# First layer of a graph network: its own-row term and offsets move into the matmul groups

## The chip, the core and the metric

The kernel runs on one core of one Trainium2 chip. The metric is device time in microseconds (us) of one launch. TensorE is written PE, VectorE DVE, ScalarE ACT, GpSimd POOL and SyncE SP. PE, DVE and ACT compute, POOL issues the gathers, SP issues most of the other transfers. Each engine works through its own instructions in the order of the program and stops at the first one whose inputs are not there.

## The reference, cut to what matters

A table of 12500 nodes with 256 features goes through a normalization, then through a graph network of three layers over 200000 edges, an attention and a mixture of experts. The change lies in the first layer of the graph network, and in how it hands its result to the second:

```python
def _sage_conv(x, src, dst, Wl, bl, Wr, num_nodes):
    msg = x[src]
    s = segment_sum(msg, dst, num_nodes)
    cnt = segment_sum(ones, dst, num_nodes)
    agg = s / maximum(cnt, 1.0)[:, None]
    return agg @ Wl.T + bl + x @ Wr.T

h = _sage_conv(xn, src, dst, Wl0, bl0, Wr0, n)
h = leaky_relu(h, 0.01)
h = _sage_conv(h, src, dst, Wl1, bl1, Wr1, n)
...
```

The **mean** term is `agg @ Wl.T`, the **own row** is `x @ Wr.T`, the **offset** is `bl`.

## The kernel before, in words

**Data.** The nodes form 98 blocks of 128 rows (`NB`), taken in 27 groups of four blocks, at the end of the order of two. The edges are sorted by target into slots of 128. In layers 1 and 2 the sums are taken after the linear product, so each layer stores two tables for the next: `y` (the product with `Wl`, which is gathered) and `z` (the product with `Wr` plus the offset, the own row). `y_tab[0]` is the normalized table itself.

**A layer** is `on_the_way_of` (L1672). Its loop (L1891) takes four slots in each step: POOL gathers four slots of messages (L1709) into a ring of 32 tiles, ACT makes the matrices `hots` that sort 128 messages into 128 targets (L1698, L1700), and PE multiplies them into the running sums `acc` (L1729). A gather into a slot waits until the product 32 slots earlier has read it. When all slots of a block have been added, `take_up` (L1742) divides the sums by the counts on DVE (L1755 to L1759) and clears them (L1767).

**Work put between the slots.** `stage(0)` takes the queue `soon`, which holds the finished groups (`products`, L697); `stage(1)` takes the queue `later`, in layer 0 the generator `first_products` (L731). Each is a generator: a step of the loop runs it to its next `yield 0.0`, one call of each per step, and a credit of `SHARE` paces the second by the costs that are yielded. So the order of instructions on every engine is written out when the program is built. Six blocks with most edges are summed differently: POOL, DVE and PE count edges per pair of nodes (`counted`, L1527) and PE multiplies the counts with the whole table (`sums`, L1651). They come in the middle and in the last third of the layer.

**`first_products`** loads a group of normalized rows, transposes it on PE (`turned`, L682, copied by ACT at L691), stores the transposed rows in `xT_tab` (L737), multiplies them with `Wr` (L744, PSUM tile `p_z`), adds the first offset on DVE (L746) and stores `z_tab[0]` (L749). `load_z` (L1788) reads that back as `h` before the group's last block is taken up.

**`products`** transposes the mean, multiplies it with `Wl` (L707, tile `p_l`), adds `h` on DVE (L710), applies the leaky ReLU on DVE (L711: the larger of `h` and 0.01 `h`), transposes the result and calls `linear`. **`linear`** (L252) multiplies with both matrices of the next layer at once into one PSUM tile `p_mm` of 512 columns (L259); ACT copies the left half (L268), DVE adds the offset to the right half (L269), and both halves are stored (L280, L281). In layer 1 the same function is called with `parts` and splits the left half in three; that branch keeps its work.

In layer 0 all PSUM tiles but `acc` and `whole` share three banks (`OneTag`, L1663). The SBUF tag `t_b` (two buffers) holds the transposed mean, the transposed `h` and the two tiles `yz` in turn; `t_a` (two buffers) holds `z0`; `h` has three buffers.

The attention already adds an offset by a product: `ones3` (3 x 128 ones, bf16) times `bo3` (three bf16 rows whose sum is the f32 offset), L845, in front of two f32 products at L847. The three rows are made at the start (L337 to L345).

Of the kernel before, what the change touches and what calls it, by code (L numbers as in the profile page):

```python
# [56 lines left out]
P = 128  # L57
D = 256
# [30 lines left out]
def gps_kernel(ctx: ExitStack, tc: tile.TileContext, x, src, dst, wlr, bl, wq, wk, wv,  # L89
# [75 lines left out]
    bo_tab = dram.tile([3, D], BF, name="bo_tab")  # L165
    xa_tab = dram.tile([NB * P, D], F32, name="xa_tab")


# [6 lines left out]
    def rows(t, b, n):  # L175

        return t[b * P:(b + n) * P, :].rearrange("(j p) d -> p j d", p=P)
# [9 lines left out]

    def spread(t):

        return bass.AP(tensor=t.tensor, offset=t.offset,  # L190
                       ap=[[0, P], [D, t.shape[0]], [1, D]])


    ident = consts.tile([P, P], F32, name="ident")
# [9 lines left out]
    nc.vector.memset(eps, EPS)  # L204


    bl_sb = consts.tile([P, 3, D], F32, name="bl_sb")
    bo3 = consts.tile([3, D], BF, name="bo3")
# [43 lines left out]
    def linear(psum, bufs, pool, layer, w, hT, b, n, parts=None):  # L252

        for j0 in range(0, n, 2):
            ps = []
            for j in range(j0, min(j0 + 2, n)):
                p = psum.tile([P, 2 * D], F32, name="p_mm", tag="p_mm", bufs=bufs)
                for k in range(2):
                    nc.tensor.matmul(p, hT[:, k, j * P:(j + 1) * P], w[:, k, :],  # L259
                                     start=(k == 0), stop=(k == 1))  # L260
# [24 lines left out]

    with ExitStack() as first:
# [47 lines left out]
        nc.scalar.dma_start(edges[E:E + P, :], fill)  # L334

        nc.sync.dma_start(bl_sb, spread(bl))
        bo = sort.tile([1, D], F32, name="bo")  # L337
        nc.sync.dma_start(bo, b_out)
        bo_parts = sort.tile([1, 3, D], BF, name="bo_parts")
        for i in range(3):  # L340
            nc.vector.tensor_copy(bo_parts[:, i, :], bo)
            if i < 2:
                nc.vector.tensor_sub(bo, bo, bo_parts[:, i, :])
        nc.sync.dma_start(bo_tab.rearrange("(o t) d -> o t d", o=1), bo_parts)
        nc.sync.dma_start(bo3, bo_tab)  # L345


        nxt_i = sort.tile([EP, 1], I32, name="nxt_i")
# [295 lines left out]
    def addresses(table, s, n, held, engine, pitch):  # L644
# [2 lines left out]
            max_val=(held - 1) * pitch, skip_runtime_bounds_check_because="clamped above")  # L647
        return at

    def finish(layer, b, n, sums, inv, work, h):  # L650


        r0 = NB - b - n
        if layer == 0:
            nc.vector.tensor_scalar(inv[:, r0:r0 + n], sums[:, :n, D], 1.0, None, op0=OP.max)
            nc.vector.reciprocal(inv[:, r0:r0 + n], inv[:, r0:r0 + n])
            m = work.tile([P, G, D], F32, name="mean", tag="t_a")
        for j in range(n):
            i = n - 1 - j
            if layer == 0:  # L660
                nc.vector.tensor_scalar(m[:, j, :], sums[:, i, :D], inv[:, r0 + i:r0 + i + 1], None,
                                        op0=OP.mult)
            else:
                nc.vector.scalar_tensor_tensor(h[:, j, :], sums[:, i, :D],
                                               inv[:, r0 + i:r0 + i + 1], h[:, j, :],
                                               op0=OP.mult, op1=OP.add)
        nc.vector.memset(sums if layer == 0 else sums[:, :n, :D], 0.0)
        if layer == 0:
            return m
        if layer == 2:  # L670
            nc.sync.dma_start(rows(z_tab[2], b, n), h[:, :n, :])
        return h
# [24 lines left out]
    def products(layer, b, n, m, h, work, psum, parts=None):  # L697


        if layer == 0:  # L700
            mT = yield from turned(m, n, work, psum, "t_b")
            for j0 in range(0, n, 2):
                nj = min(2, n - j0)
                p = psum.tile([P, 2, D], F32, name="p_l", tag="p_mm", bufs=2)
                for j in range(j0, j0 + nj):
                    for k in range(2):
                        nc.tensor.matmul(p[:, j - j0, :], mT[:, k, j * P:(j + 1) * P],  # L707
                                         wlr_sb[:, 0, k, :D], start=(k == 0), stop=(k == 1))
# [22 lines left out]
    def first_products(b, n, work, psum):  # L731

        xn = work.tile([P, G, D], F32, name="xn", tag="t_d")
        nc.sync.dma_start(xn[:, :n, :], rows(y_tab[0], b, n))
        yield 0.0
        xT = yield from turned(xn, n, work, psum, "t_c")
        nc.sync.dma_start(xT_tab[:, :, b * P:(b + n) * P], xT[:, :, :n * P])  # L737
        z = work.tile([P, G, D], F32, name="z0", tag="t_a")
        for j0 in range(0, n, 2):
            nj = min(2, n - j0)  # L740
            p = psum.tile([P, 2, D], F32, name="p_z", tag="p_mm", bufs=2)
            for j in range(j0, j0 + nj):
                for k in range(2):
                    nc.tensor.matmul(p[:, j - j0, :], xT[:, k, j * P:(j + 1) * P],  # L744
                                     wlr_sb[:, 0, k, D:], start=(k == 0), stop=(k == 1))
            nc.vector.tensor_add(z[:, j0:j0 + nj, :], p[:, :nj, :],  # L746
                                 bl_sb[:, 0:1, :].to_broadcast([P, nj, D]))
# [86 lines left out]
    def attended(b, n, work, psum):  # L834
# [6 lines left out]
        for j0 in range(0, n, 2):  # L841
            nj = min(2, n - j0)
            p = psum.tile([P, 2, D], F32, name="p_a", tag="p_mm", bufs=2)
            for j in range(j0, j0 + nj):
                nc.tensor.matmul(p[:, j - j0, :], ones3, bo3, start=True, stop=False)  # L845
                for k in range(2):
                    nc.tensor.matmul(p[:, j - j0, :], xT[:, k, j * P:(j + 1) * P], m2_sb[:, k, :],  # L847
                                     start=False, stop=(k == 1))
            nc.vector.tensor_add(xa[:, j0:j0 + nj, :], xa[:, j0:j0 + nj, :], p[:, :nj, :])
            yield 0.9 * nj  # L850
# [473 lines left out]
    def one_by_one():  # L1324

        with ExitStack() as stack:
# [6 lines left out]
            with ExitStack() as inner:  # L1333
# [5 lines left out]
                for layer in range(3):  # L1339
# [8 lines left out]
                    for b, n in falling:  # L1348
# [5 lines left out]
                        h = work.tile([P, G, D], F32, name="h")  # L1354
                        nc.sync.dma_start(h[:, :n, :], rows(z_tab[layer], b, n))
# [316 lines left out]
    def on_the_way_of(layer, table, last, work, psum, inv, msgs, a, c, e):  # L1672
# [109 lines left out]
        def load_z(g):  # L1782
            b, n = falling[g]
            if g >= group_of[FEWER] and not e:
                zs[g] = c.work.tile([P, 2, D], F32, name="h_c", bufs=PAIRS)
            else:
                zs[g] = work.tile([P, G, D], F32, name="h", bufs=3)
            nc.sync.dma_start(zs[g][:, :n, :], rows(z_tab[layer], b, n))  # L1788

        def ask(g):  # L1790

# [197 lines left out]
```

## Time and profile before

| what | value |
| --- | --- |
| five runs | 6685.4 to 6712.27 us, median 6687.13 us |
| profiled execution, its own time | 6699.41 us |
| its span in the profile | 6697.6 us |
| mean clock that PE was granted | 0.883 |
| layer 0 | about 190 us to 2345 us of the span |
| `first_products` in it | 192 us to 640 us |
| `products` of layer 0 | 302 us to 2336 us |

A row of the group view names line, engine and operation, the tile written, the tiles read, the shape (partitions x elements), the count, the busy time in us, the mean ns of one, and the idle time ahead of it with what ended that idle time. An f32 product of the program is two MATMULs in the trace (392 for 196 at L744), a bf16 product is one. "The chain" is the chain of work that ended last, followed back from the end; its shares are shares of the time in the window asked for. PEclk is the share of the full clock that PE was granted.

### The profile page before, as it was taken

What the parts mean: (1) busy time and instruction counts of PE and PEld (TensorE: products, weight loads), DVE (VectorE), ACT (ScalarE), POOL (GpSimd) and SP (SyncE); (2) the same over time, 40 slices, a digit from 0 to 9 for tenths busy, and PEclk for the clock granted to TensorE, in tenths of its full rate; (3) what the DMA queues carried; (4) which work ended last, traced back from release to release, by engine and by line L of the source; (5) the groups of instructions that cost most, each with busy time, mean ns of one, the idle gap of its engine ahead of it and who ended that gap; (6) DMA issues with size and microseconds to landing.
All of it is one profiled execution on the core that took longest, in us unless ns stands there. A gap on an engine that the chain in (4) does not pass through costs nothing.

```text
span 6697.6 us, 77095 instructions
## 1 busy us (share of the span) xinstructions
PE 5107.5 (76%) x23443; PEld 3722.4 (56%) x23443; DVE 2179.4 (33%) x6539; ACT 2252.7 (34%) x5187; POOL 4077.1 (61%) x4243
## 2 busy tenths in 40 slices
PE   1567677678888867877878776588889877888878
PEld 0446455455776645655555554356666545666556
DVE  6426647464000112222111100134444423333333
ACT  3324333344333334444333333122232222322223
POOL 1566667676666565665655666566666655666563
PEclk9879889889999979888888887689999888999889
DMA  6546334445777555555666654555666645666442
GB/s 200 159 136 201 109 111 128 123 151 177 228 225 226 178 163 185 182 175 178 208 219 207 213 165 138 169 178 178 196 183 201 181 131 159 187 184 182 148 148 81
DMA packets 752785, 1154.11 MB, mean 172 GB/s; under 512 B 109813, under 2 KB 582800, under 8 KB 752134
## 3 DMA queue, kind: packets, MB, share of 16 engines
q0 software_dynamic: 218320, 616.79, 31.3%
q1 hardware_dynamic: 516489, 512.20, 23.6%
q10 hardware_dynamic: 17578, 20.04, 0.9%
q8 instruction: 221, 3.62, 0.2%
q14 instruction: 177, 1.45, 0.1%
HBM read 940.73 MB, written 207.91 MB: 171 GB/s over the span
## 4 chain that ended last, share of the span: by engine, by line
PE 59%; issue 12%; another core or an unknown queue 11%; DVE 7%; ACT 6%; DMA 3%; POOL 2%; SPq 0%; ACTq 0%; DVEq 0%; POOLq 0%
PE acc L1729 19%; PE whole L1651 8%; PE p_h L1246 7%; PE p_y L1214 7%; PE p_mm L259 4%; ACT hots L1698 2%; PE p_n L1561 2%; PE p_tr L682 2%; PE p_a L847 1%; POOL msg L1709 1%; PE p_l L707 1%; ACT hots L1700 1%; PE p_z L744 1%; PE p_b L946 1%
## 5 line engine op out<-in xcount | busy, mean ns | idle before, releaser
L1709 POOL DMA_INDIRECT msg<-y,src_of x2480 | 2427.9, 979 | 1472.2 <-issue 653.8
L1709 POOL DMA_INDIRECT msg_parts<-y_parts,src_of x1404 | 1400.0, 997 | 726.0 <-issue 362.1
L1729 PE MATMUL acc<-msg,hots 128*128 128x257 f32 (+1 forms) x4960 | 1428.4, 410 | 501.2 <-issue 290.8
L1729 PEld LDWEIGHTS acc<-msg,hots 128*128 128x128 f32 x4960 | 975.8, 205 | 747.4 <-issue 421.4
L1698 ACT ACTIVATE hots<-cols,dst_of 128x128 f32<-128x128 f32 x2480 | 789.3, 391 | 740.2 <-remote 319.9
L1651 PE MATMUL whole<-y_c,count 128*128 128x256 f32 x2744 | 754.7, 396 | 60.9 <-issue 43.9
L1729 PE MATMUL acc<-msg_parts,hots 128*128 128x256 bf16 x4212 | 655.0, 284 | 126.7 <-issue 77.7
L1214 PE MATMUL p_y<-w_sb,hT 128*128 128x256 f32 x2368 | 599.1, 396 | 83.6 <-DVE x L1201 31.5
L1729 PEld LDWEIGHTS <-hots 128*128 128x128 bf16 x4212 | 424.3, 102 | 423.3 <-issue 296.4
L1246 PE MATMUL p_h<-turned,w_sb 128*128 128x512 f32 (+1 forms) x1344 | 620.9, 588 | 28.5 <-issue 17.1
L1651 PEld LDWEIGHTS whole<-y_c,count 128*128 128x128 f32 x2744 | 539.3, 200 | 160.4 <-issue 82.8
L1248 ACT ACTIVATE hT<-p_h,b_sb 128x512 f32<-128x512 f32 (+1 forms) x336 | 211.5, 636 | 1007.5 <-PE p_h L1246 434.5
L1214 PEld LDWEIGHTS p_y<-w_sb,hT 128*128 128x128 f32 x2368 | 448.6, 199 | 162.0 <-issue 37.5
L1700 ACT ACTIVATE hots<-hots,ones 128x512 f32<-128x512 f32 x620 | 447.4, 722 | 20.2
L1703 DVE TENSOR_TENSOR hots<-cols,dst_of 128x512 bf16<-128x512 f32 x351 | 240.7, 687 | 638.4 <-PE acc L1729 351.5
L1201 DVE SCALAR_TENSOR_TENSOR x<-p_y,comb,x 128x256 f32<-128x256 f32 x592 | 257.0, 476 | 515.4 <-PE p_y L1214 176.4
L259 PE MATMUL p_mm<-wlr_sb,turned 128*128 128x512 f32 x784 | 383.1, 632 | 52.6 <-issue 19.4
L1561 PE MATMUL p_n<-dst_hot,src_hot 128*128 128x256 bf16 x2058 | 299.3, 290 | 112.5 <-issue 75.1
L1246 PEld LDWEIGHTS p_h<-turned,w_sb 128*128 128x128 f32 x1344 | 255.2, 208 | 190.1 <-issue 165.0
L1561 PEld LDWEIGHTS <-src_hot 128*128 128x128 bf16 x2058 | 212.0, 104 | 200.1 <-issue 133.3
L691 ACT COPY turned<-p_tr 128x512 f32<-128x512 f32 (+1 forms) x204 | 105.5, 546 | 535.6 <-PE p_tr L682 255.2
L1541 DVE TENSOR_SCALAR src_hot<-nums,source_of 128x384 bf16<-128x384 uint16 x693 | 226.7, 327 | 177.5 <-remote 122.3
(386 smaller groups left out, 4633.9 us busy)
## 6 DMA issues: line engine op xcount, KB each, us to landing
count<-counts SPq DMA_DIRECT2D x294, 256.0 KB
y_c<-y SPq DMA_DIRECT2D x294, 256.0 KB
msg<-y,src_of POOLq DMA_INDIRECT x2480
counts<-counts_sb SPq DMA_DIRECT2D x96, 384.0 KB
h<-z SPq DMA_DIRECT2D x66, 512.0 KB
z<-yz SPq DMA_DIRECT2D x98, 256.0 KB
xT<-xT_tab SPq DMA_DIRECT2D x44, 512.0 KB
msg_parts<-y_parts,src_of POOLq DMA_INDIRECT x1404
```

What stands on the lines that cost most here:

```text
L259: nc.tensor.matmul(p, hT[:, k, j * P:(j + 1) * P], w[:, k, :], start=(k == 0), stop=(k == 1))
L1201: nc.vector.scalar_tensor_tensor(xt[:, j, :], p[:, j - j0, :], comb[:, j, i:i + 1], xt[:, j, :], op0=OP.mult, op1=OP.add)
L1214: nc.tensor.matmul(p[:, j - j0, :], hT[:, k, j * P:(j + 1) * P], e.w2[:, i, k, :], start=(k == 0), stop=(k == 1))
L1246: nc.tensor.matmul(p_h[:, :n * P], e.w1[:, i, k, m * P:(m + 1) * P], tT[:, k, :n * P], start=(k == 0), stop=(k == 1))
L1541: nc.vector.tensor_scalar(src_hot[:, i, :], self.nums, source[:, c:c + 1], None, op0=OP.is_equal)
L1561: nc.tensor.matmul(p[:, t, :], s_hot[:, (t0 + t) * P:(t0 + t + 1) * P], d_hot, start=(i == 0), stop=(i == len(mine) - 1))
L1651: nc.tensor.matmul(acc[:, h * D:(h + 1) * D], c[:, j, h * P:(h + 1) * P], y[:, j, :], start=False, stop=True, skip_group_check=True)
L1698: nc.scalar.activation(hot[:, i, :], cols, AF.Abs, bias=dst_of[:, s + i:s + i + 1], scale=-1.0)
L1700: nc.scalar.activation(hot[:, :n, :], hot[:, :n, :], AF.Relu, bias=ones[:, 0:1], scale=-1.0)
L1703: nc.vector.tensor_tensor(hot[:, :n, :], cols.rearrange("p (o c) -> p o c", o=1).to_broadcast([P, n, P]), dst_of[:, s:s + n].rearrange("p ...
L1709: got = nc.gpsimd.indirect_dma_start(out=msgs[s % held] if e else msgs[s % held][:, :D], out_offset=None, in_=y_parts if e else y_tab[laye ...
L1729: got = nc.tensor.matmul(sums, hot, msgs[s % held][:, k * D:k * D + w], start=False, stop=True, skip_group_check=True)
```

## The change

- `first_products` ends with the store of `xT_tab`. Its product with `Wr`, the addition and the store of `z_tab[0]` go.
- `load_h` reads, in layer 0, the group's transposed rows from `xT_tab` in place of `z_tab[0]`, into the same three buffers.
- `products` of layer 0 builds one PSUM group for each block: the offset as `ones3` x `rows3`, two products of the own row, two of the mean. ACT writes 0.01 times the PSUM tile to a new tile `h0` (tag `t_a`), DVE takes the larger of PSUM and `h0`. The pair of blocks now ends with `yield 0.0`, so a group of four takes one more call of `stage(0)`.
- `linear`, called without `parts`, adds the offset as `ones3` x `rows3` between its two products of a block, and ACT copies all 512 columns. The addition on DVE goes there.
- At the start, the two offsets and the attention's offset are split together as one row of 768 in place of 256, with one more load; `bl_sb` keeps the third offset alone.

```diff
@@ linear
                 for k in range(2):
                     nc.tensor.matmul(p, hT[:, k, j * P:(j + 1) * P], w[:, k, :],
                                      start=(k == 0), stop=(k == 1))
+                    if k == 0 and not parts:
+                        nc.tensor.matmul(p[:, D:], ones3, rows3[:, layer, :], start=False,
+                                         stop=False, skip_group_check=True)
...
-                nc.scalar.copy(y3[:, j, 0, :] if parts else yz[:, j, :D], p[:, :D])
-                nc.vector.tensor_add(yz[:, j, D:], p[:, D:], bl_sb[:, layer, :])
+                if not parts:
+                    nc.scalar.copy(yz[:, j, :], p)
+                    continue
+                nc.scalar.copy(y3[:, j, 0, :], p[:, :D])
+                nc.vector.tensor_add(yz[:, j, D:], p[:, D:], bl_sb)
@@ start
-        bo_parts = sort.tile([1, 3, D], BF, name="bo_parts")
+        row = sort.tile([1, 3 * D], F32, name="row")
+        nc.sync.dma_start(row[:, :2 * D], bl[0:2, :].rearrange("(o l) d -> o (l d)", o=1))
+        nc.sync.dma_start(row[:, 2 * D:], b_out)
+        row_parts = sort.tile([1, 3, 3 * D], BF, name="row_parts")
...
+    def load_h(h, layer, b, n):
+        if layer == 0:
+            nc.sync.dma_start(h[:, :, :n * P], xT_tab[:, :, b * P:(b + n) * P])
+        else:
+            nc.sync.dma_start(h[:, :n, :], rows(z_tab[layer], b, n))
@@ products
         if layer == 0:
+            xT, h = h, work.tile([P, G, D], F32, name="h0", tag="t_a")
             mT = yield from turned(m, n, work, psum, "t_b")
...
                 for j in range(j0, j0 + nj):
-                    for k in range(2):
-                        nc.tensor.matmul(p[:, j - j0, :], mT[:, k, j * P:(j + 1) * P],
-                                         wlr_sb[:, 0, k, :D], start=(k == 0), stop=(k == 1))
+                    nc.tensor.matmul(p[:, j - j0, :], ones3, rows3[:, 0, :], start=True,
+                                     stop=False)
+                    for i, (vT, side) in enumerate(((xT, slice(D, 2 * D)), (mT, slice(0, D)))):
+                        for k in range(2):
+                            nc.tensor.matmul(p[:, j - j0, :], vT[:, k, j * P:(j + 1) * P],
+                                             wlr_sb[:, 0, k, side], start=False,
+                                             stop=(i + k == 2))
                 hs = h[:, j0:j0 + nj, :]
-                nc.vector.tensor_add(hs, hs, p[:, :nj, :])
-                nc.vector.scalar_tensor_tensor(hs, hs, SLOPE, hs, op0=OP.mult, op1=OP.max)
-                yield 0.9 * nj
-            yield 0.0
+                nc.scalar.activation(hs, p[:, :nj, :], AF.Copy, scale=SLOPE)
+                nc.vector.tensor_tensor(hs, p[:, :nj, :], hs, OP.max)
+                yield 1.9 * nj
+                yield 0.0
@@ first_products
         nc.sync.dma_start(xT_tab[:, :, b * P:(b + n) * P], xT[:, :, :n * P])
-        z = work.tile([P, G, D], F32, name="z0", tag="t_a")
-        for j0 in range(0, n, 2):
-            nj = min(2, n - j0)
-            p = psum.tile([P, 2, D], F32, name="p_z", tag="p_mm", bufs=2)
-            for j in range(j0, j0 + nj):
-                for k in range(2):
-                    nc.tensor.matmul(p[:, j - j0, :], xT[:, k, j * P:(j + 1) * P],
-                                     wlr_sb[:, 0, k, D:], start=(k == 0), stop=(k == 1))
-            nc.vector.tensor_add(z[:, j0:j0 + nj, :], p[:, :nj, :],
-                                 bl_sb[:, 0:1, :].to_broadcast([P, nj, D]))
-            yield 0.9 * nj
-        nc.sync.dma_start(rows(z_tab[0], b, n), z[:, :n, :])
```

More of the change, by code (lines that the diff above doesn't have):

```diff
@@ L164, in gps_kernel @@
     xT_tab = dram.tile([P, 2, NB * P], F32, name="xT_tab")
-    bo_tab = dram.tile([3, D], BF, name="bo_tab")
+    rows_tab = dram.tile([3, 3 * D], BF, name="rows_tab")
     xa_tab = dram.tile([NB * P, D], F32, name="xa_tab")
@@ L188, in spread @@
     def spread(t):
-        return bass.AP(tensor=t.tensor, offset=t.offset,
-                       ap=[[0, P], [D, t.shape[0]], [1, D]])
+        return bass.AP(tensor=t.tensor, offset=t.offset + 2 * D, ap=[[0, P], [1, D]])
     ident = consts.tile([P, P], F32, name="ident")
@@ L204, in gps_kernel @@
     nc.vector.memset(eps, EPS)
-    bl_sb = consts.tile([P, 3, D], F32, name="bl_sb")
-    bo3 = consts.tile([3, D], BF, name="bo3")
+    bl_sb = consts.tile([P, D], F32, name="bl_sb")
+    rows3 = consts.tile([3, 3, D], BF, name="rows3")
     ones3 = consts.tile([3, P], BF, name="ones3")
@@ L336, in gps_kernel @@
         nc.sync.dma_start(bl_sb, spread(bl))
-        bo = sort.tile([1, D], F32, name="bo")
-        nc.sync.dma_start(bo, b_out)
-        bo_parts = sort.tile([1, 3, D], BF, name="bo_parts")
+        row = sort.tile([1, 3 * D], F32, name="row")
+        nc.sync.dma_start(row[:, :2 * D], bl[0:2, :].rearrange("(o l) d -> o (l d)", o=1))
+        nc.sync.dma_start(row[:, 2 * D:], b_out)
+        row_parts = sort.tile([1, 3, 3 * D], BF, name="row_parts")
         for i in range(3):
-            nc.vector.tensor_copy(bo_parts[:, i, :], bo)
+            nc.vector.tensor_copy(row_parts[:, i, :], row)
             if i < 2:
-                nc.vector.tensor_sub(bo, bo, bo_parts[:, i, :])
-        nc.sync.dma_start(bo_tab.rearrange("(o t) d -> o t d", o=1), bo_parts)
-        nc.sync.dma_start(bo3, bo_tab)
+                nc.vector.tensor_sub(row, row, row_parts[:, i, :])
+        nc.sync.dma_start(rows_tab.rearrange("(o t) d -> o t d", o=1), row_parts)
+        nc.sync.dma_start(rows3, rows_tab.rearrange("t (l d) -> t l d", l=3))
         nxt_i = sort.tile([EP, 1], I32, name="nxt_i")
@@ L844, in attended @@
             for j in range(j0, j0 + nj):
-                nc.tensor.matmul(p[:, j - j0, :], ones3, bo3, start=True, stop=False)
+                nc.tensor.matmul(p[:, j - j0, :], ones3, rows3[:, 2, :], start=True, stop=False)
                 for k in range(2):
@@ L1353, in one_by_one @@
                         r0 = NB - b - n
-                        h = work.tile([P, G, D], F32, name="h")
-                        nc.sync.dma_start(h[:, :n, :], rows(z_tab[layer], b, n))
+                        h = work.tile([P, 2, G * P] if layer == 0 else [P, G, D], F32, name="h")
+                        load_h(h, layer, b, n)
                         m = finish(layer, b, n, aggv[:, r0:r0 + n], inv, work, h)
@@ L1786, in load_z @@
             else:
-                zs[g] = work.tile([P, G, D], F32, name="h", bufs=3)
-            nc.sync.dma_start(zs[g][:, :n, :], rows(z_tab[layer], b, n))
+                zs[g] = work.tile([P, 2, G * P] if layer == 0 else [P, G, D], F32, name="h",
+                                  bufs=3)
+            load_h(zs[g], layer, b, n)
         def ask(g):
```

## Prediction

> **What bounds the kernel now.** The change touches layer 0 alone, 190 to 2345 us of a span of 6697.6. I read the chain of waits of the page first, for the lines that end last, then the same chain in windows of the layer, the busy time by window, and the group view for durations.
>
> ```profile
> span 6697.6 us, 77095 instructions
> PE 59%; issue 12%; another core or an unknown queue 11%; DVE 7%; ACT 6%; DMA 3%; POOL 2%; SPq 0%; ACTq 0%; DVEq 0%; POOLq 0%
> ```
>
> PE carries the chain. That it does so in layer 0 too, and not POOL with its gathers, I take from a count: instructions of the gather (L1709) and of the product that uses it (L1729), from the start to two moments, by the windows view of each line.
>
> ```profile
> 0.00:1200.00 1200.00, 556.85 (x536) 0.86 0.49 148
> 0.00:2200.00 2200.00, 1180.79 (x1164) 0.89 0.55 168
> ```
>
> ```profile
> 0.00:1200.00 1200.00, 298.97 (x1016) 198.22 (x1016) 0.86 0.49 148
> 0.00:2200.00 2200.00, 668.33 (x2272) 438.25 (x2272) 0.89 0.55 168
> ```
>
> A product is two MATMULs, so 508 products stand against 536 gathers, later 1136 against 1164: POOL is 28 slots ahead both times, and its ring holds 32. POOL is always nearly out of free slots. The order of work on PE, with what PE waits for, sets the pace.
>
> ```profile
> core 0: us, PE busy (x) PEld busy (x) DVE busy (x) ACT busy (x) POOL busy (x), PEclk, DMA share, GB/s
> 190.00:645.00 455.00, 316.27 (x1698) 243.09 (x1696) 187.27 (x476) 152.36 (x379) 276.37 (x285) 0.84 0.57 173
> 645.00:1000.00 355.00, 233.89 (x1082) 170.62 (x1083) 201.30 (x547) 120.47 (x299) 230.41 (x235) 0.80 0.37 108
> 1000.00:1350.00 350.00, 255.47 (x1365) 181.94 (x1363) 212.92 (x754) 129.40 (x323) 250.64 (x213) 0.88 0.42 126
> 1350.00:1660.00 310.00, 242.11 (x1312) 179.00 (x1311) 168.74 (x623) 145.71 (x368) 208.14 (x202) 0.91 0.53 161
> 1660.00:2345.00 685.00, 590.35 (x2460) 471.97 (x2460) 63.40 (x165) 251.51 (x645) 413.47 (x438) 0.94 0.68 215
> ```
>
> Three stages: A (190 to 645) holds `first_products`, B (645 to 1660) the counting, where DVE is over half busy, C (1660 to 2345) the sums by counts, where PE is busy 86% and DVE 9%. The chain in A and in C:
>
> ```profile
> by line: issue 20.2%; PE acc L1729 15.5%; PE p_z L744 15.1%; POOL msg L1709 9.1%; PE p_mm L259 6.1%; PE p_tr L682 5.7%; another core or an unknown queue 5.2%; PE p_l L707 3.9%; DVE z L746 2.8%; PE whole L1454 2.6%; DVE got_runs L1501 2.1%;
> ```
>
> ```profile
> by line: PE whole L1651 35.1%; PE acc L1729 26.5%; issue 8.9%; another core or an unknown queue 7.6%; PE p_mm L259 7.4%; PE p_l L707 4.6%; DMA y_c<-y 1.9%; PE p_tr L682 1.8%; ACT hots L1698 1.8%; DMA msg<-y,src_of 0.9%; ACT hots L1700 0.8%;
> ```
>
> **The change part by part.** *Own row leaves A.* On the chain stand p_z with 15.1% of 455 us, 69 us of its 99 busy, and the addition L746 with 2.8%, 13 us of 34. Both go: -82 us. POOL could follow: 285 instructions of about 0.96 + 0.30 us need 359 of the 455 us.
>
> *Own row comes back in `products`.* As many matmuls (392 in the trace), same shape as those of the mean (L707: 104 us busy), standing directly beside them in the same PSUM group. So they get the chain share of p_l: 3.9% of 455 in A (18 us), 5.3% of 645 to 1000 (19 us), some 2 us to 1350, 3.6% to 1660 (11 us), 4.6% of C (32 us): +82 us of 104. The two cancel on the chain; the work merely moves from A, which has idle PE time, to C, which has nearly none.
>
> *Offsets as products.* 196 small matmuls are new, 98 in `products` and 98 in `linear`. The trace has the very form at L845, and its price is the spacing, not its 0.28 us of duration. Timeline of the attention:
>
> ```profile
> 3332.36 0.28 PE L845 MATMUL p_a<-bo,ones 3*128 3x256 bf16 x1
> 3332.57 1.13 PE L847 MATMUL p_a<-m_sb,xT 128*128 128x256 f32 x4
> 3333.64 0.28 PE L845 MATMUL p_a<-bo,ones 3*128 3x256 bf16 x1
> ```
>
> A block takes 1.27 us from one L845 to the next. Four f32 MATMULs without it take 0.86: sixteen of p_l go through in 3.45 us on the chain. So one offset costs 0.41 us, though only three rows deep, since the change between bf16 and f32 spreads its neighbours. In `linear` it stands between MATMULs of 512 columns, under which a weight load hides better; bounds 0.2 (its own slot in the lines above) and 0.41, taken 0.3. That is 98 x 0.41 + 98 x 0.3 = 40 + 29 us of PE. Of p_l 82 of 104 us are on the chain (79%), of p_mm 122 of 185 (6.1%, 4.2% and 7.4% of A, B and C; 66%): 32 + 19 = **+51 us**.
>
> The Trainium skill prices this lower: "TensorE: Matmul & The Clock Gate", section "Back-to-back issue gap", gives an isolated warm matmul N / 2.4 + 2.5 ns, 109 ns for 256 columns. By that estimate 196 offsets are 21 us of PE and the whole sum would end within 0.3% of no change. The 1.27 us per block at L845 contradict it for this mixture of types, so the row is used.
>
> *Leaky ReLU.* The addition L710 (0.69 us a pair) and L711 (0.69) become an ACT copy with a scale (L688 has the same form from PSUM: 0.60) and a DVE maximum (L689: 0.69). The path from PE to the transposes is 0.09 us shorter in each of 49 pairs, but the PSUM bank is held 0.60 us longer, and the first step now waits in ACT's queue. Behind it ACT has the `hots` of three steps ahead, so there is cover. Taken 0; ends -34 (49 x 0.69, all of L711) and +29 (49 x 0.60).
>
> *`linear` evicted whole.* ACT's copy grows from 0.37 to 0.59 us (L268 against L691), 98 times, +21 us of ACT, which is 37% busy; DVE loses 98 x 0.42 = 41 us. PE waited for L269 24 us in all (15.8 at the transposes, 8.2 at p_n). Taken -8; ends -24 and +21.
>
> *Transfers.* 27 stores of z go. The load of `h` has the same size, from `xT_tab`. PE now waits for it instead of DVE, in front of the products of the next slots; but it is asked for 16 slots ahead. On the chain of A it stood with 12.7 us. Taken -3; ends -13 and +13. The SP queue is shorter by the 27 stores.
>
> *Start and end.* The five DVE instructions on the split row take 3 x 0.274 + 2 x 0.406 = 1.6 us now and at most three times that; one more load waits on SP. +3, ends 0 and +5. Before layer 1 can gather, the last group must be through: two blocks x (0.86 + 0.7), +3. The extra call of `stage(0)` for each group delays only that group, and there are eight or more steps per group of four: nothing.
>
> *Gain of A.* A removed piece gives its full length only until another wait ends last; A has DVE, POOL and transfers close behind. I take off 4 us.
>
> Sum: -82 + 82 + 51 + 0 - 8 - 3 + 3 + 3 + 4 = **+50 us**. Against the profiled execution's 6699.41 us this is 6749; against the median of the runs, 12 us lower, **6737 us** (+0.75%).
>
> On the clock: PE had 0.84 of it in A and 0.94 in C, so work leaves a stage of lower clock and each matmul is cheaper where it goes; inside the 0.86 us above this is not counted. The Trainium skill ("TensorE: Matmul & The Clock Gate", "HAM oscillation — how this bites in real kernels") has the other side, a PE that waits often falls to half rate: if A without p_z lost as much clock as its emptiest 100 us show (0.67), its other 217 us of PE would take some 55 us longer, and the sum would be near +100.
>
> **Rivals.** *Faster: the added work falls into gaps.* PE is idle for 28% of B, and what ends last there is DVE (the two hot matrices and the sorting). If PE's additions vanish in those gaps and DVE, 109 us lighter in the layer (34 + 41 + 34), gives back more than I took, the sum is -82 in A, +18 + 14 for the own rows and offsets there, +5 in B less 20 for DVE, +32 for C: -33, **6654 us**. It decides from the share of the new PE work on the path: of 104 + 69 us, less than 82, 47%. Against it: p_l stands on the chain with 79% already.
>
> *No change.* The own row moves free of charge, the offsets cost 0.2 us each (39 us, 27 of it on the path), and all 24 us that PE waited for L269 come back: -82 + 82 + 27 - 24 = +3, **6690 us**.
>
> *Much slower.* The relief of A is taken by the transfers and the sorting behind it (half of the 82 gained), and every new matmul and the longer hold of the three PSUM banks is paid: -41 + 104 + 69 = +132 less 20 for DVE, **6800 us**.
>
> *The change does not do what it says:* if the new order let `first_products` run at the same pace with fuller steps, A would not shorten. That is the rival above; 285 POOL instructions against 455 us speak against it.
>
> **How the numbers follow.** Forecast (+20 to +105) 0.60; faster 0.15; no change 0.17; much slower 0.08. About 0.3%, 20 us, is what a measurement of this kernel can tell from no change. The range takes the upper ends (own rows fully paid +22, offsets at 0.41 all paid +80) to 6790, and downward the faster rival to 6655. Faster by over 0.3%: 0.15; within: 0.17; slower: 0.68.
>
> **What would show it.** `first_products` ends some 40 to 55 us earlier; in C the time grows by about 50 us with PE busier than 86%; p_l has 784 f32 MATMULs and its groups of four blocks take 8.5 us instead of 3.45; an offset in `linear` adds 0.2 to 0.41 us to the spacing. The lead of POOL stays near 28. If the lead falls below 20 in A, POOL has become the bound there and the gain is cut. If C does not grow, or B shrinks, the forecast is wrong, and the faster rival right.

## The result, and the profile after

The changed kernel takes 6721.5 us (median of 37 runs, 6691 to 6754), the kernel before in runs beside it 6696.7 (63 runs): a ratio of **1.004, with an interval of 1.0029 to 1.005**, 19 to 33 us slower. The forecast was +50. Two repeats beside the experiments gave 1.0037 (1.0022 to 1.0053) and 1.0039 (1.0022 to 1.0057).

The profile page of the changed kernel, the two lines that answer to those of before:

```profile
span 6716.4 us, 77141 instructions
PE 57%; another core or an unknown queue 14%; issue 12%; ACT 6%; DVE 6%; DMA 3%; POOL 1%; SPq 0%; DVEq 0%; ACTq 0%; POOLq 0%
```

PE carries the chain as before. The counts of gathers (L1715 now) and of the MATMULs that use them (L1735), by the windows view of each line:

```profile
0.00:1200.00 1200.00, 564.83 (x544) 0.86 0.46 139
0.00:2200.00 2200.00, 1171.09 (x1160) 0.89 0.53 161
```

```profile
0.00:1200.00 1200.00, 308.65 (x1040) 206.28 (x1040) 0.86 0.46 139
0.00:2200.00 2200.00, 668.59 (x2266) 438.59 (x2266) 0.89 0.53 161
```

544 against 520, 1160 against 1133: POOL is 24 and 27 slots ahead, nearly as before.

To compare stages I cut both traces at the same work instead of the same time: the starts of the 1st, 249th, 807th, 1240th and 1241st gather. The 249th is near the end of `first_products`, the 807th near the start of C, the 1241st is the first gather of layer 1. First the kernel before, then the changed one (columns as in the prediction: length, busy times of PE, PEld, DVE, ACT and POOL with counts, PEclk):

```profile
177.12:645.06 467.94, 319.51 (x1708) 245.99 (x1708) 197.14 (x527) 159.10 (x395) 287.25 (x295) 0.85 0.56 170
645.06:1658.05 1012.99, 731.47 (x3756) 531.56 (x3756) 582.90 (x1922) 395.52 (x988) 687.54 (x646) 0.86 0.43 130
1658.05:2311.36 653.31, 569.89 (x2383) 458.46 (x2384) 57.91 (x154) 235.12 (x601) 409.91 (x433) 0.94 0.70 221
2311.36:2339.53 28.17, 20.45 (x78) 13.51 (x76) 5.49 (x11) 13.92 (x39) 0.95 (x1) 1.00 0.21 62
```

```profile
182.53:630.59 448.06, 289.29 (x1443) 197.18 (x1444) 153.66 (x455) 167.33 (x401) 285.30 (x294) 0.80 0.49 148
630.59:1654.49 1023.90, 788.17 (x4038) 559.35 (x4037) 544.48 (x1843) 416.74 (x1016) 684.77 (x646) 0.87 0.43 129
1654.49:2325.51 671.02, 604.31 (x2530) 475.17 (x2531) 35.92 (x109) 246.60 (x610) 409.27 (x433) 0.95 0.69 216
2325.51:2361.17 35.66, 28.50 (x112) 18.62 (x110) 4.79 (x11) 17.49 (x46) 0.95 (x1) 0.98 0.16 47
```

A second trace of before and two more of the changed kernel came with the experiments. Together (us; the last column sorts the terms of the recorded prediction by stage, for A and B roughly):

| stage | before | changed | difference of means | recorded |
| --- | --- | --- | --- | --- |
| start (to the first gather) | 177, 178 | 183, 182, 182 | +4 | +3 |
| A | 468, 458 | 448, 437, 444 | -20 | about -50 |
| B | 1013, 1026 | 1024, 1027, 1034 | +9 | about +45 |
| C | 653, 659 | 671, 669, 672 | +15 | about +50 |
| end of layer 0 | 28, 29 | 36, 35, 34 | +6 | +3 |

The signs are right, and A, B and C move by a fifth to two fifths of what was forecast. The sum, +14, is below the measured +25; the stretch from there to a late gather some 90 us before the end, which the change leaves alone, took 4271 and 4284 us before and 4269, 4260 and 4303 after, so single traces do not settle ten microseconds.

The pieces themselves are as the diff says: in the group view p_l has 392 + 368 + 24 = 784 f32 MATMULs and 98 offsets. The timeline of two blocks in C:

```profile
1720.49 0.28 PE L720 MATMUL p_l<-rows,ones 3*128 3x256 bf16 x1
1720.70 1.13 PE L724 MATMUL p_l<-wlr_sb,h 128*128 128x256 f32 x4
1721.67 1.03 PE L724 MATMUL p_l<-wlr_sb,turned 128*128 128x256 f32 x4
1722.63 0.28 PE L720 MATMUL p_l<-rows,ones 3*128 3x256 bf16 x1
1722.84 1.13 PE L724 MATMUL p_l<-wlr_sb,h 128*128 128x256 f32 x4
1723.80 1.03 PE L724 MATMUL p_l<-wlr_sb,turned 128*128 128x256 f32 x4
1724.67 0.60 PE L1735 MATMUL acc<-msg,hots 128*128 128x257 f32 x2
```

A block takes 2.14 us. Eight f32 MATMULs alone take 2 x 0.86 = 1.72, so the offset costs 0.42. In `linear` the copies of ACT follow PE block by block; the last two of the layer, before and changed:

```profile
2334.17 0.37 ACT L268 COPY yz<-p_mm 128x256 f32<-128x256 f32 x1 [1.80 <-PE p_mm L259]
2335.89 0.37 ACT L268 COPY yz<-p_mm 128x256 f32<-128x256 f32 x1 [1.34 <-PE p_mm L259]
```

```profile
2355.50 0.58 ACT L271 COPY yz<-p_mm 128x512 f32<-128x512 f32 x1 [2.21 <-PE p_mm L258]
2357.63 0.58 ACT L271 COPY yz<-p_mm 128x512 f32<-128x512 f32 x1 [1.54 <-PE p_mm L258]
```

They stand 1.72 us apart before and 2.13 now: 0.41 for the offset here too.

### The profile page after: what moved, and what is told of

It is laid out like the page before. It is cut to its first block, busy times and chain, and to the rows that moved or that the text cites. A ratio compares the mean times of both kernels' runs of the same rounds, so it can differ in the third digit from the quotient of the medians.

```text
span 6716.4 us, 77141 instructions
## 1 busy us (share of the span) xinstructions
PE 5172.6 (77%) x23639; PEld 3726.9 (55%) x23639; DVE 2074.5 (31%) x6343; ACT 2296.4 (34%) x5236; POOL 4073.0 (61%) x4243
## 4 chain that ended last, share of the span: by engine, by line
PE 57%; another core or an unknown queue 14%; issue 12%; ACT 6%; DVE 6%; DMA 3%; POOL 1%; SPq 0%; DVEq 0%; ACTq 0%; POOLq 0%
PE acc L1735 18%; PE whole L1657 8%; PE p_y L1220 7%; PE p_h L1252 7%; PE p_mm L258 4%; ACT hots L1704 2%; PE p_l L724 2%; PE p_n L1567 2%; PE p_tr L695 2%; ACT hots L1706 1%; POOL msg L1715 1%; PE p_a L853 1%; PE p_s L1113 1%; PE p_b L952 1%
## 5 line engine op out<-in xcount | busy, mean ns | idle before, releaser
L1715 POOL DMA_INDIRECT msg<-y,src_of x2480 | 2423.9, 977 | 1488.1 <-issue 685.4
L1715 POOL DMA_INDIRECT msg_parts<-y_parts,src_of x1404 | 1400.3, 997 | 725.9 <-issue 359.0
L1735 PE MATMUL acc<-msg,hots 128*128 128x257 f32 (+1 forms) x4960 | 1434.9, 412 | 495.6 <-issue 228.6
L1735 PEld LDWEIGHTS acc<-msg,hots 128*128 128x128 f32 x4960 | 983.7, 207 | 740.9 <-issue 404.0
L1735 PE MATMUL acc<-msg_parts,hots 128*128 128x256 bf16 x4212 | 653.5, 283 | 121.6 <-issue 82.0
L1735 PEld LDWEIGHTS <-hots 128*128 128x128 bf16 x4212 | 423.9, 102 | 411.1 <-issue 285.3
L1252 PE MATMUL p_h<-turned,w_sb 128*128 128x512 f32 (+1 forms) x1344 | 604.7, 574 | 30.0 <-issue 24.2
L258 PE MATMUL p_mm<-wlr_sb,turned 128*128 128x512 f32 x784 | 409.2, 646 | 60.7 <-DVE yz L278 24.2
L1769 DVE SCALAR_TENSOR_TENSOR h<-acc,inv_w,h 128x256 f32<-128x256 f32 x188 | 90.7, 483 | 559.3 <-remote 310.9
```

The lines of the kernel that those rows point to most:

```text
L1252: nc.tensor.matmul(p_h[:, :n * P], e.w1[:, i, k, m * P:(m + 1) * P], tT[:, k, :n * P], start=(k == 0), stop=(k == 1))
L1715: got = nc.gpsimd.indirect_dma_start(out=msgs[s % held] if e else msgs[s % held][:, :D], out_offset=None, in_=y_parts if e else y_tab[laye ...
L1735: got = nc.tensor.matmul(sums, hot, msgs[s % held][:, k * D:k * D + w], start=False, stop=True, skip_group_check=True)
```

## The experiments

They ran on four chips. On two the kernel before takes 6695 and 6752 us, like the 6697 above; on the other two it takes 5614 and 5609. I call them the slower and the faster chips; a kernel is only compared with the kernel before on its own chip. The faster ones turned out to be the clearer witnesses.

**Without the offsets** (faster chip).

```diff
-                    if k == 0 and not parts:
-                        nc.tensor.matmul(p[:, D:], ones3, rows3[:, layer, :], start=False,
-                                         stop=False, skip_group_check=True)
...
-                    nc.tensor.matmul(p[:, j - j0, :], ones3, rows3[:, 0, :], start=True,
-                                     stop=False)
...
```

> The changed kernel without its 196 offset products; both offsets of the first two layers are left out of the result. By the timeline of the changed kernel one costs 0.41 us of PE in both places (blocks of p_l 2.14 us apart where eight f32 MATMULs take 1.72; ACT's copies of p_mm 2.13 apart where they were 1.72), 80 us of PE in all. Recorded working (79% and 66% of it on the path): 32 + 27 = 59 us less than the changed kernel, some 30 us below the kernel before. Theory of gaps and clock (PE's added work falls for half into idle time, and a busier PE runs at a higher clock): 25 to 40 us less than the changed kernel, within 15 us of the kernel before. If the offsets are hidden: no more than 10 us less.

Measured: 0.9998 of before (0.9989 to 1.0007). That is within 15 us of before, as the theory of gaps has it, and not the 30 below of the recorded working.

**The move of the own row alone** (faster chip).

```diff
+                    for i, (vT, side) in enumerate(((xT, slice(D, 2 * D)), (mT, slice(0, D)))):
...
-                nc.vector.tensor_add(hs, hs, p[:, :nj, :])
+                nc.vector.tensor_add(hs, p[:, :nj, :], bl_sb[:, 0:1, :].to_broadcast([P, nj, D]))
                 nc.vector.scalar_tensor_tensor(hs, hs, SLOPE, hs, op0=OP.mult, op1=OP.max)
...
```

The cut parts are those of the change: `load_h` reads `xT_tab`, and `first_products` ends with the store of `xT_tab`.

> The kernel before with the move of the own row alone: products of the own row beside those of the mean, the offset added by DVE from PSUM, leaky ReLU and linear as before, no offset products. Recorded working: -82 in the first stage and +82 later, so 0 within 10 us. If the loss of the change lies in the move (the first stage gives back less than was taken out, since its other matmuls run at a lower clock): 15 to 30 us slower than before. If both stages return half (40 off, 40 on), also 0, but then the first stage is only some 20 us shorter in the profile, and the later ones only some 20 us longer, instead of 64 and 64.

Measured: 1.0013 (1.0004 to 1.0022), 7 us slower. This lies inside the 10 us of the recorded working, but not for its reason: the table below has A at 376 us without p_z in it, and at 375 with p_z kept.

**Without the own row** (both faster chips, one after the other).

```diff
-  for i, (vT, side) in enumerate(((xT, slice(D, 2 * D)), (mT, slice(0, D)))):
+  for i, (vT, side) in enumerate(((mT, slice(0, D)),)):
...
```

> The changed kernel without the 196 products of the own row in products (392 MATMULs); the own row is left out of the result, its load stays. The MATMULs held PE for 102 us in the changed kernel. Recorded working: 79% of it on the path, 82 us less than the changed kernel, about 55 below the kernel before. Theory of gaps and clock: 35 to 60 us less than the changed kernel; the counting stage, where PE is idle a quarter of the time, gives back under half of its 49 us, and its other matmuls get slower per piece.

> Once more the changed kernel without its products of the own row (left out of the result), since its first run was on a chip on which both kernels take 5614 us. There the last stage gave back 29 us of the 26 that 120 MATMULs need, the counting stage nothing. On a chip where the kernel before takes 6690: recorded working 82 us less than the changed kernel (0.991 of the time before). Theory of gaps: the last stage and the last group give back 25 to 30 us, the first two stages 0 to 15, so 25 to 45 us less than the changed kernel, 0.997 to 1.000 of the time before.

Measured: 0.9989 (0.998 to 0.9998) and 0.9987 (0.9978 to 0.9996), 6 and 7 us below before. The expectations count from the changed kernel, which did not run on these chips; the next experiment stands in for it.

**p_z kept in A** (faster chip).

```diff
         nc.sync.dma_start(xT_tab[:, :, b * P:(b + n) * P], xT[:, :, :n * P])
...
+            p = psum.tile([P, 2, D], F32, name="p_z", tag="p_mm", bufs=2)
...
+                    nc.tensor.matmul(p[:, j - j0, :], xT[:, k, j * P:(j + 1) * P],
+                                     wlr_sb[:, 0, k, D:], start=(k == 0), stop=(k == 1))
```

> The changed kernel with the 392 MATMULs of p_z left in first_products, their result read by nobody (no addition, no store of z). Recorded working: the first stage grows by the 69 us that stood on its chain, the kernel is 96 us slower than before. Theory of clock: the first stage grows by 20 to 40 us only, since the gather products there go back from 295 to about 260 ns of PE's time each as the granted clock returns from 0.79 to about 0.84; the kernel is 45 to 65 us slower than before.

Measured: 1.0054 (1.0041 to 1.0067), 30 us slower than before. This lies under both expectations of the whole kernel, and stage A says why. Windows between the same gathers in A, without the own row (first fence) and with p_z kept, which also has its own rows (second):

```profile
183.49:557.82 374.33, 269.82 (x1416) 185.25 (x1417) 172.98 (x482) 176.61 (x423) 285.86 (x294) 0.88 0.59 178
```

```profile
181.45:556.14 374.69, 334.85 (x1844) 254.59 (x1844) 159.43 (x461) 170.00 (x410) 286.24 (x294) 0.97 0.59 178
```

428 more MATMULs, 65 us more of busy PE, and A is 0.4 us longer. The theory of the clock in the expectation is visible (0.88 becomes 0.97, a MATMUL of the gathered messages holds PE for 250 ns instead of 283, from its start to the next one's or to its own end) but it does not set the time. POOL does: its waits in that stage, in the kernel without the own row, are only the 0.30 us after each gather (waits: us in all, times, longest).

```profile
POOL msg L1715 <- issue: 69.5, 228, 0.3
POOL got_runs L1482 <- issue: 12.4, 41, 0.3
POOL msg L1715 <- DMA y<-o_norm: 12.3, 1, 12.3
```

286 us busy and 294 x 0.30 = 88 us give 374: **POOL's floor**, and A stands on it to the microsecond. (The 12.3 us wait lies in front of the first gather, outside the stage.) The same sum for the other stages is 685 + 646 x 0.30 = 879 in B and 410 + 433 x 0.30 = 540 in C. All traces of the faster chips (us):

| kernel | A | B | C | end |
| --- | --- | --- | --- | --- |
| without own row (two chips) | 374, 375 | 881, 880 | 547, 550 | 22, 22 |
| without offsets | 374 | 876 | 555 | 24 |
| own row moved alone | 376 | 889 | 560 | 21 |
| p_z kept | 375 | 877 | 581 | 28 |
| features on partitions, p_z kept (below) | 376 | 889 | 544 | 16 |

A and B stand on POOL's floor whatever PE has to do (in the 889 us POOL is busy 693, 8 to 13 more than in the others); only C and the end follow PE. The kernel before has no trace on these chips; that p_z is free in A there rests on the last two rows. In C PE is the bound, as the windows of the kernels without the own row, without the offsets and with p_z kept show:

```profile
1438.57:1985.34 546.77, 545.48 (x2419) 439.12 (x2418) 36.61 (x110) 251.66 (x621) 410.20 (x433) 1.00 0.82 258
```

```profile
1430.75:1985.83 555.08, 553.78 (x2507) 466.11 (x2506) 37.68 (x114) 255.68 (x631) 409.30 (x434) 1.00 0.81 256
```

```profile
1433.04:2014.29 581.25, 577.68 (x2558) 467.38 (x2559) 37.69 (x114) 252.66 (x622) 410.06 (x433) 0.99 0.79 247
```

PE is busy for all but 1 to 4 us. The own row costs 581 - 547 = 34 us in C and 7 at the end, the offsets 581 - 555 = 26 and 5. By the runs: own row and p_z 1.0054 - 0.9989 = 36 us, offsets and p_z 1.0054 - 0.9998 = 31 us, of 80 us of PE for the offsets.

**Both kernels unaltered, and before without p_z** (a slower chip).

```diff
...
-                    nc.tensor.matmul(p[:, j - j0, :], xT[:, k, j * P:(j + 1) * P],
-                                     wlr_sb[:, 0, k, D:], start=(k == 0), stop=(k == 1))
-            nc.vector.tensor_add(z[:, j0:j0 + nj, :], p[:, :nj, :],
-                                 bl_sb[:, 0:1, :].to_broadcast([P, nj, D]))
+            nc.vector.tensor_copy(z[:, j0:j0 + nj, :],
+                                  bl_sb[:, 0:1, :].to_broadcast([P, nj, D]))
```

> The changed kernel itself, unaltered, beside the experiments on their chip. The result gave 1.004. If p_z costs nothing in the first stage where POOL sets the pace (with and without it the 434th gather starts within 1 us), the changed kernel should stand some 25 us above the kernel before there too (1.003 to 1.006). If the relief of the first stage is worth 20 to 70 us, as in the recorded working, it stands below 1.002.

> The kernel before itself, for its trace beside the others of this call. Where POOL sets the pace of the first stage, its 434th gather starts within 5 us of that of the changed kernel; where PE does, 13 us later or more, as in the first pair of traces.

> The kernel before without the 392 MATMULs of p_z; DVE writes the offset alone to z, so the own row is left out of the result. Recorded working: 69 us of them stood on the chain of the first stage, so 65 to 70 us less than before. Theory: the first stage has another bound close behind (POOL's gathers, stops that no work fills, and a lower clock for what is left), so 0 to 20 us less.

Measured: the changed kernel 1.0037, before without p_z **0.9978 (0.9962 to 0.9993): 15 us, not 69**. The 434th gather starts 7 us earlier in the changed kernel than in before, between the two expectations: PE has some say here. Stage A of before and of before without p_z, same chip, one trace each (the two traces of before differ by 10 us in A):

```profile
178.43:636.65 458.22, 324.05 (x1708) 246.16 (x1708) 196.87 (x527) 159.39 (x395) 287.23 (x295) 0.86 0.57 173
```

```profile
178.96:618.07 439.11, 257.74 (x1316) 183.62 (x1316) 181.34 (x524) 158.63 (x390) 287.68 (x295) 0.78 0.59 181
```

392 MATMULs that held PE for 96 us are gone, and the stage is 19 us shorter. PE's busy time falls by 66 only: the granted clock goes from 0.86 to 0.78, a MATMUL of the messages holds PE for 312 ns instead of 265, and 30 us come back that way. The other 47 us are idle time of PE. POOL's floor is 287 + 88 = 375 us; the stage stands 82 us above it before and 63 without p_z. So on this chip the floor is not what A came to rest on. The longest waits of PE and of DVE in that stage without p_z say what stood there instead:

```profile
PE acc L1724 <- DVE mean L1754: 39.0, 3, 33.0
PE p_tr L682 <- DVE h L710: 33.8, 2, 32.0
```

```profile
DVE inv_w L1750 <- remote: 82.7, 4, 49.3
DVE h L710 <- remote: 53.3, 1, 53.3
```

Two single waits for DVE hold PE for 33 and 32 us, and DVE itself stood 49 and 53 us until "remote", a release by nothing that the profile knows. Whether these waits grew because p_z went, one trace cannot say.

**`linear` alone** (the same slower chip).

```diff
+                    if k == 0 and not parts:
+                        nc.tensor.matmul(p[:, D:], ones3, rows3[:, layer, :], start=False,
+                                         stop=False, skip_group_check=True)
...
-                nc.scalar.copy(y3[:, j, 0, :] if parts else yz[:, j, :D], p[:, :D])
-                nc.vector.tensor_add(yz[:, j, D:], p[:, D:], bl_sb[:, layer, :])
+                    nc.scalar.copy(yz[:, j, :], p)
```

> The kernel before with the change of linear alone: its offset as 98 small products and ACT copying all 512 columns; own row, leaky ReLU and first_products as before. Recorded working: +19 for the offsets, -8 for the copies: 11 us slower. Theory: an offset costs 0.41 us, but only where PE sets the pace (30 blocks of the last stage and the 2 of the last group, 13 us), and nothing in the first two stages: 5 to 15 us slower. If the lighter DVE is worth more than that: 5 to 10 us faster.

Measured: 1.0026 (1.0009 to 1.0043), 17 us slower, between 6 and 29. The recorded +11 and most of the theory's 5 to 15 lie inside; a gain by the lighter DVE does not.

**A version that keeps p_z and drops the transposing of h** (a faster and a slower chip). The own row is cheap in A and dear in C, so it stays in A; both products are written with features on partitions.

```diff
-                    nc.tensor.matmul(p[:, j - j0, :], mT[:, k, j * P:(j + 1) * P],
-                                     wlr_sb[:, 0, k, :D], start=(k == 0), stop=(k == 1))
+                    nc.tensor.matmul(p[:, :n * P], wlr_sb[:, 0, k, f * P:(f + 1) * P],
+                                     mT[:, k, :n * P], start=(k == 0), stop=(k == 1))
...
-        hT = yield from turned(h, n, work, psum, "t_b", leaky=layer == 1)
+            hT = h
...
```

> A version made from the kernel before: own row and offset stay in the first stage, but both products of the first layer are written with features on partitions, so the offset is a column that DVE adds while it evicts p_z, and h needs no transposing (196 transposes on PE, some 0.13 us each, and 50 copies on ACT go, 0.6 us of waiting at the end). Theory: what counts is PE's work in the last stage, where 60 transposes stood, 8 us, and the shorter way from the mean to linear: 5 to 25 us below the kernel before. By the recorded working (66 to 79% of all PE work): 17 to 21 us below. If the counting stage or POOL set the end, within 5 us of before.

Measured: 0.9992 (0.9983 to 1.0001), 4 us below before: less than the first two expectations, inside the third, in which POOL sets the end. Its stage C:

```profile
1444.36:1988.22 543.86, 527.24 (x2284) 431.32 (x2283) 59.32 (x160) 234.91 (x596) 411.92 (x434) 0.99 0.82 260
```

POOL's floor there is 412 + 434 x 0.30 = 542: PE is busy 527 of 544 us and no longer sets the stage. By this sum more relief of PE would buy nothing in C on this chip; no run tried it.

> The changed kernel unaltered, once more, for whichever chip this call gets. Where the kernel before takes 5610 us: the same kernel with p_z kept stood 30 us above before and p_z cost nothing in the first stage there, so 1.004 to 1.006; if p_z did cost its share there (20 us or more), 1.000 to 1.002. Where it takes 6690 us: 1.003 to 1.005 as before.

> The version with features on partitions, once more. Where the kernel before takes 5610 us: 4 us below it as in the first run, within 5. Where it takes 6690 us and every wait of PE for another engine can be a stop of some 10 us: the shorter chain from the mean to linear has one wait less in each of 27 groups, so 10 to 40 us below before; if only PE's work counts, 5 to 15 us below; 0 if the counting stage's other waits take its place.

On a slower chip the changed kernel gave 1.0039 and this version 0.9981 (0.996 to 1.0002), 13 us below before by the ratio, and 36 below the changed kernel by the medians on the same chip. The interval does not part the expectations. Of the kernels that compute everything it has the lowest median wherever it ran, though neither interval leaves 1; the unaltered changed kernel was not run on a faster chip.

## Why the prediction was right in sign and twice too large

**Own row leaves A, -82.** This step failed. Its 69 us for p_z measured 15 (5 to 25) on a slower chip and nothing on a faster one. I took the share that p_z has on the chain as the gain of removing it. A chain names what happened to end last; it does not say how close the next bound is. On a faster chip the row that would have told was in the text: POOL needs 359 us. I used it as room for A to shorten and took 4 us off for "another wait"; there it was the floor. On a slower chip, where the forecast was made and measured, the floor left 82 us of room and does not explain the 15. There a third of the 96 us came back as slower matmuls (30 us), and half stood as idle time of PE (47 us), with the two long waits for DVE shown above. The chain of A had a sign of it: 20.2% "issue" and 5.2% "another core or an unknown queue", which I passed over.

**Own row comes back +82, offsets +51.** The same error with the other sign. From before without p_z to the changed kernel it is 1.0037 - 0.9978 = 40 us, where the terms make 69 + 50 = 119. On the faster chips the own row in `products` is paid in C and at the end alone, 34 + 7 us, and so are the offsets, 26 + 5. Of the 40 us on the slower chips only the 17 of `linear` were measured by themselves; 23 are left for the rest by difference. Two errors of one kind, on opposite signs, cancelled to a large part: that the forecast came out right in sign is in part luck.

**Price of an offset.** 0.41 us in `products` was right (0.42). In `linear` I took 0.3 of bounds 0.2 and 0.41; it is 0.41. My reason for the price, the change between bf16 and f32, was wrong, as lines of the kernel before show:

```profile
801.40 1.25 PE L1561 MATMUL p_n<-dst_hot,src_hot 128*128 128x256 bf16 x10 [0.20 <-DVE src_hot L1541]
802.49 0.60 PE L1729 MATMUL acc<-msg,hots 128*128 128x257 f32 x2
802.92 1.15 PE L1561 MATMUL p_n<-dst_hot,src_hot 128*128 128x256 bf16 x9
```

```profile
4482.49 0.82 PE L1729 MATMUL acc<-msg_parts,hots 128*128 128x256 bf16 x6
4483.24 1.13 PE L946 MATMUL p_b<-b_sb,combT 32*128 32x256 f32 x4
4484.30 0.50 PE L1729 MATMUL acc<-msg_parts,hots 128*128 128x256 bf16 x3
```

In the first three lines the type changes twice at 128 rows, and it costs nothing: ten bf16 MATMULs take 1.09 us, two f32 ones 0.43. In the next three the number of rows changes too, from 128 to 32 and back. Six bf16 MATMULs now take 0.75 us instead of 0.65 and four f32 ones 1.06 instead of 0.86: 0.3 us more in all, as much as an offset costs beyond its own slot of 0.11. So the price goes with the change in rows (3 among 128), not in type; no run varied the rows of the offset itself.

The rule of the Trainium skill ("TensorE: Matmul & The Clock Gate", "Back-to-back issue gap") that I weighed against the row gives 109 ns for 256 columns. The trace agrees where the rows stay 128 (1.09 us for ten) and not for the offset; the row decides. As a sum of times its 21 us are near the 31 us measured, but for another reason: on the faster chips PE's full price is paid in C and at the end and nowhere else.

**The clock.** The same page's "HAM oscillation — how this bites in real kernels" was right in kind: with less work in A, PE ran at 0.78 to 0.83 there instead of 0.85 or 0.86. It returned 30 of 96 us as slower matmuls. It did not push the kernel near +100: A became shorter all the same.

**The rest.** Start +4 for +3. The end +6 for +3: from the last mean to the first gather of layer 1 it is 13.3 us before and 16.1 now, the +3 as forecast; the other 3 lie in the slots ahead of it. Leaky ReLU by ACT and DVE: from the last MATMUL of the layer's last group to h 1.45 us before and 1.35 now, nearly nothing, as taken. The loads of the transposed rows were not tried by themselves; nothing in the traces waits for them.

**What was to show it.** PE in C is busier than 86% (90%; between the same gathers 87% before), the lead stays near 28, p_l is as said (two pairs of blocks, 4.2 us each), the offset in `linear` is at the upper bound. `first_products` was to end 40 to 55 us earlier; its last store ends at 626 us instead of 640. C was to grow by 50 us, and grew by 15. Of the rivals, faster and much slower did not come. The time lies midway between "no change" (+3) and the forecast, but not by that rival's reasons: the offset costs its 0.41 us and the move is not free.

**The lead of POOL.** 24 to 28 slots ahead was read rightly and led me wrong. On a faster chip, without the own row, the lead is 3 to 11 slots in most of A and B and 22 to 28 in most of C (counted every 100 us): there the ring is full in the stage that PE sets. On the slower chips it is nearly full in all stages; I take late signals to be the reason. The timeline of before, just behind A, where PE's transposes of the mean are over by 657.4:

```profile
656.34 1.04 PE L682 MATMUL p_tr<-ident,mean 128*128 128x128 f32 x8
...
668.26 1.07 ACT L691 COPY turned<-p_tr 128x512 f32<-128x512 f32 x2 [15.93 <-remote]
668.63 0.94 POOL L1709 DMA_INDIRECT msg<-y,src_of  x1 [3.89 <-remote]
668.89 1.65 PE L707 MATMUL p_l<-wlr_sb,turned 128*128 128x256 f32 x3 [9.78 <-ACT turned L691]
```

ACT's copy starts 11 us after the matmuls it needs, released by something that the profile does not know, and POOL and PE stand meanwhile. No work on PE stands in this wait, so I see no saving on PE that would remove it. That the 63 to 82 us above POOL's floor in A come from such stops is my reading of these lines and of the two long waits above; which share of them PE's work could still move was not separated.

## What to carry to other kernels

Before a chain share becomes a gain, add up the next engine's own time in that stage, issue slots included: the distance to that floor caps what the removal can give, and the same holds for work that is added. On the faster chips this cap was all; on the slower it allowed 82 us where 15 came, so it bounds a gain and does not give it: only the run without p_z gave it. Price work by the stage where it lands: moved out of a stage near POOL's floor and into one where PE is busy all the time, it cost its full duration and returned little (faster chips). A full ring shows who is late now, not who would be late next.

## What the runs showed of the hardware that was not expected

- The same kernel before takes 5609 to 5614 us on two chips and 6695 to 6752 us on others, at a mean granted clock of about 0.95 against 0.88. In the waits view of every slower trace, idle time released by "remote" adds up to 2340 to 2800 us over all engines; in the six traces of the faster chips there is none. What delays the signals on a program with one core stays open, and each chip was measured at one time only, so whether this stays with a chip is not shown.
- The granted clock follows PE's load within one stage, both ways: 0.86 to 0.78 with 96 us of matmuls taken from A, 0.88 to 0.97 with p_z and own rows added there.
- A product of few rows among products of 128 rows costs some 0.3 us of PE beyond its own slot, for 3 bf16 rows and for 32 f32 rows alike; the change between bf16 and f32 at 128 rows costs nothing (109 ns and 216 ns a MATMUL on either side of it).
- POOL's gathers in B take 1074 to 1084 ns on average in before, in the own row moved alone, without p_z and in the version with features on partitions, and 1056 to 1069 in the changed kernel and its relatives, in which DVE has less to do; `linear` alone has 1071. Over 558 gathers that is some 8 us of POOL's floor. The Trainium skill ("SBUF — State Buffer", "Who interferes with whom") has DVE and GpSimd share a port pair, so this may be the cause; no run here singled out the DVE instruction.
